# Transformer scores on 64 rows: queries and keys as exact halves in float32r, projected transposed, with their maxima turned by TensorE

## The chip, the core and the metric

One core of a Trainium2 chip runs the whole program. Its engines work side by side: TensorE (PE) multiplies matrices and writes the result to PSUM (8 banks of 512 float32 on each of 128 partitions), VectorE (DVE) and ScalarE (ACT) empty PSUM into SBUF, GpSimd (POOL) works on SBUF alone, and SyncE (SP) issues most of the DMAs. Every engine takes its instructions in a fixed order and waits on semaphores. TensorE's array can be cut: four pieces of 32 rows or two of 64 rows work at once on matmuls with few rows, and four pieces of 32 columns on matmuls with few outputs. The metric is device time from the first to the last instruction, in microseconds; before the change it is 3513.88 us, the median of three runs (3512.74 to 3514.75).

## The reference, cut to what matters

The program is a chain of eight residual stages on x of shape [2, 512, 128]: slot attention, a mixture of experts, cross-attention, a LoRA feed-forward, a six-layer transformer, a quantised feed-forward, a second six-layer transformer of the same form, and a second mixture of experts. The change is in the two transformers, of which each layer is:

```python
NL, D, H, DFF = (6, 128, 16, 512)
HD = D // H                                   # 8 per head
def _attn(q, k, v, mask):
    scores = jnp.einsum('bqhd,bkhd->bhqk', q, k) / np.float32(np.sqrt(HD))
    scores = jnp.where(mask[:, None, None, :], jnp.float32(-jnp.inf), scores)
    w = jax.nn.softmax(scores, axis=-1)
    return jnp.einsum('bhqk,bkhd->bqhd', w, v)
for i in range(NL):
    xn = _adaln(x, noise_emb, n1_w[i], n1_b[i])
    q, k, v = jnp.split(xn @ qkv_w[i].T, 3, axis=-1)
    q, k = _rope(q.reshape(B, L, H, HD)), _rope(k.reshape(B, L, H, HD))
    x = x + _attn(q, k, v.reshape(B, L, H, HD), src_mask).reshape(B, L, D) @ so_w[i].T
    xn = _adaln(x, noise_emb, n2_w[i], n2_b[i])
    q = _rope((xn @ cq_w[i].T).reshape(B, L, H, HD))
    k = _rope((context @ ck_w[i].T).reshape(B, LC, H, HD))
    v = (context @ cv_w[i].T).reshape(B, LC, H, HD)
    x = x + _attn(q, k, v, ctx_mask).reshape(B, L, D) @ co_w[i].T
    xn = _adaln(x, noise_emb, n3_w[i], n3_b[i])
    h = jax.nn.gelu(xn @ f1_w[i].T + f1_b[i], approximate=False)
    x = x + (h @ f2_w[i].T + f2_b[i])
```

There are 2 sequences of 512 tokens (B, L), 154 context tokens (LC) and 16 heads of 8 numbers. A layer so has two own-attentions and two cross-attentions, one for each sequence.

## The kernel before

**An attention block** (class Block) belongs to one sequence and works on 16 heads in four groups of four (class Group). A score has only 8 products, so the four heads of a group lie on four stretches of 32 partitions of qT and kT, and four matmuls run on the array at once. Each group passes over its scores twice. `maximum` computes them with queries on the output's partitions, 512 keys (own) or two times 154 keys (cross) to a bank, and VectorE reduces each bank to the negated maxima of 128 queries. `close` turns these maxima with a VectorE transpose and puts them by four small DMAs into one of the 32 rows of qT, against a row of ones in kT. `exp` then computes the scores anew with keys on the output's partitions, where that row subtracts the maximum, and ScalarE writes the exponentials to tiles p. When all chunks of keys of a group are done (4 of 128, or 2 of 77), 16 or 8 matmuls with the values vp or vcp, 32 output columns for each head, add up into one bank; `finish` transposes it on VectorE, divides by the sum that a column of ones gave, and writes the tile a.

**Around the groups** `before` makes the normalised input xn (layer norm on VectorE with a power on GpSimd, four TensorE transposes, scale and shift on ScalarE into nrm_t) and projects it to keys and queries. A projection is four matmuls with tokens on the output's partitions; `rope` multiplies it by cosines and sines on VectorE (rope_a, rope_s) and joins them on GpSimd (turned); `to_rows` transposes 32x32 blocks on VectorE (rows) and sends them by four DMAs to the rows of qT or kT. `context` does the same for the keys of the context, by way of kcp, TensorE transposes and ScalarE copies to kcT. `after` turns a, projects it, adds it to Y and, in a cross block, does the feed-forward layer.

**The order** is worked out when the program is built. The transformer runs two chains, the maxima of all groups and, LAG = 22 steps behind, their exponents, and records every instruction. The class Plan then orders the recorded instructions of all engines by a model of their durations, of the buffers and of the array's shapes, with shifts by kind of instruction (SHIFTS, by names such as "sync dma_start qT<rows"), and flushes them: all these instructions have the one source line 413. In a transformer all eight PSUM banks are one pool, ms. The layer's weights lw are one tile of 2826 columns in two buffers, loaded by one DMA. Before the transformers, `fixtures` sets aside and clears the tiles that both keep (vp, vcp, kcp, qT, kT), and `fix` fills in the mask row and the row of ones.

Of the kernel before, what the change touches and what calls it, by code (L numbers as in the profile page):

```python
# [12 lines left out]
F32 = mybir.dt.float32  # L13
U32 = mybir.dt.uint32
# [8 lines left out]
B = 2  # L23
# [8 lines left out]
NEG = -1e30  # L32
NL, H, HD, HG = 6, 16, 8, 4
DFF = 512
# [13 lines left out]
for _n, _w in (("n1", 256), ("n2", 256), ("n3", 256), ("q", 128), ("k", 128), ("v", 128), ("so", 128),  # L48
               ("cq", 128), ("ck", 128), ("cv", 128), ("co", 128), ("f1", 512), ("f2", 512),
               ("nb", 6), ("f1b", 4)):  # L50
    LAYER[_n] = slice(_at, _at + _w)
    _at += _w
LAYER_W = _at
LEAD, LAG, STEP = 30.0, 22, 0.9
MASK, TOP = 1, 31
# [17 lines left out]
PAIRS = ((0,), (1,), (2,), (3,)), ((2,), (3,), (0,), (1,))  # L73
# [3 lines left out]
for _n, _w in (("iota", 512), ("iota_p", NT), ("cos", NT * 4), ("sin", NT * 4), ("cos_c", NC * 4), ("sin_c", NC * 4), ("mask_row", 1)):  # L77
    CONST[_n] = slice(_at, _at + _w)
    _at += _w
# [39 lines left out]
class Op:  # L119
# [4 lines left out]
    def __init__(self, plan, lane, method, a, k):  # L124
# [16 lines left out]
        if lane == "tensor":  # L141
            cols = self.out[0].free_size()
            one = 0.838 * cols
            self.takes, self.lands = (max(one, 107.0), 170.0) if method == "transpose" else (2 * max(one, 55.0), 170.0)
            lhs = self.ins[0]
            (rows, r), (cells, c) = self.span(lhs), self.span(self.out[0])
# [37 lines left out]
class Plan:  # L184
# [76 lines left out]
    def order(self):  # L261
# [50 lines left out]
        cells = [0.0] * 16  # L312
# [11 lines left out]
        def place(x):  # L324
# [12 lines left out]
            if op.cells:  # L337
                s = max(s, max(cells[c] for i in sets[x] for c in ops[i].cells)) if op.mode == mode else max(s, max(cells) + self.SWITCH)
            elif op.table and op.table != table and s - at[x] < self.PATIENCE:
                s += self.TABLE  # L340
            return s

        while len(out) < n:
# [11 lines left out]
            for i in sets[x]:  # L355
# [6 lines left out]
                if op.cells:  # L362
                    last = max(cells[c] for c in op.cells)
                    s = max(s, last)
# [36 lines left out]
    def flush(self):  # L401
        order, where = self.order()

        def put(x):

            if isinstance(x, bass.AP) and x.tensor.name in where:
                return bass.AP(self.rooms[x.tensor.name].places[where[x.tensor.name]].tensor, x.offset, x.ap)
            return x
# [8 lines left out]
class Kernel:  # L417
    def __init__(self, ctx, tc, io):
# [10 lines left out]
        self.ctx_tok = c.tile([CP, B * NC, D], F32, name="ctx_tok")  # L429
# [5 lines left out]
        self.k = c.tile([P, CONST_W], F32, name="k")  # L435
        nc.sync.dma_start(self.k, io["consts"])
# [9 lines left out]
        for stages, banks in (((self.context, self.stage0, self.stage1, self.stage2, self.fixtures, self.weights5, self.stage3, self.fix), wide), ((self.stage4,), deep),  # L446
# [58 lines left out]
    def add_back(self, dst, ps, bias=None, ev=1):  # L505

        nc = self.nc
        t = self.ln.tile([P, S], F32, name="back")
# [9 lines left out]
    def normed(self, b, src, name="nrm"):  # L518

        t = self.ln.tile([P, NT, D], F32, name=name)  # L520
        self.layernorm(t, src[:, b * NT:(b + 1) * NT, :], P, NT)
        return t
# [36 lines left out]
    def stage0(self):  # L559
        nc, X = self.nc, self.X  # L560
        scale = math.sqrt(D)
        with self.pool("s0", 1) as one, self.pool("s0w", 2) as two:
# [36 lines left out]
            with nc.stretch():  # L599
                for b in range(B):  # L600
                    tok = slice(b * NT, (b + 1) * NT)
                    nc.at(0.0)
                    slots = self.normed(b, X, name=f"slots{b}")
# [4 lines left out]
                    for it in range(3):  # L608
# [47 lines left out]
                        slots = self.normed(0, s1c, name=f"slots{b}")  # L656
# [17 lines left out]
    def one_hot(self, out, idx):  # L674

        self.nc.vector.tensor_tensor(out, self.k[:, CONST["iota"]][:, 0:8].unsqueeze(1).to_broadcast([P, T, 8]),
                                     idx.unsqueeze(2).to_broadcast([P, T, 8]), ALU.is_equal)
# [216 lines left out]

    def rope(self, pool, dst, ps, cos, sin, rows, n):

        nc = self.nc
        x = ps.rearrange("p (n g f) -> p n g f", n=n, f=4)
        a = pool.tile([P, NT, 2 * H, 4], F32, name="rope_a")[:rows, :n]
        s = pool.tile([P, NT, 2 * H, 4], F32, name="rope_s")[:rows, :n]  # L900
        nc.vector.tensor_tensor(a, x, cos.unsqueeze(2).to_broadcast([rows, n, 2 * H, 4]), ALU.mult)
        nc.vector.tensor_tensor(s, x, sin.unsqueeze(2).to_broadcast([rows, n, 2 * H, 4]), ALU.mult)
        a, s = (t.rearrange("p n (h two) f -> p n h two f", two=2) for t in (a, s))
        nc.gpsimd.tensor_tensor(dst[0], a[:, :, :, 0, :], s[:, :, :, 1, :], ALU.subtract)
        nc.gpsimd.tensor_tensor(dst[1], a[:, :, :, 1, :], s[:, :, :, 0, :], ALU.add)
# [21 lines left out]
    def fixtures(self):  # L927
# [3 lines left out]
        self.tf = self.ctx.enter_context(self.pool("tf", 1))  # L931
        self.Y = self.tf.tile([P, T, D], F32, name="Y")
        self.qT, self.kT, self.kcp, self.vp, self.vcp, self.mx = ([] for _ in range(6))
        for b in range(B):
            for lst, name, rows, shape in ((self.kcp, "kcp", CP, [NC, H, 32]), (self.vp, "vp", P, [NT, VW]), (self.vcp, "vcp", CP, [NC, VW]),
                                           (self.mx, "mx", P, [32])):
                t = self.tf.tile([rows, *shape], F32, name=f"{name}{b}")
                nc.gpsimd.memset(t, 0.0)
                lst.append(t)
            for lst, name in ((self.qT, "qT"), (self.kT, "kT")):  # L940
                lst.append(self.tf.tile([P, HG, S], F32, name=f"{name}{b}"))

    def fix(self):

        nc = self.nc
        with self.pool("fix", 1) as one:
            at = CONST["mask_row"].start
            fixed = one.tile([P, NT, HG, 32], F32, name="fixed")
            nc.gpsimd.memset(fixed, 0.0)
            nc.vector.memset(fixed[:, :, :, TOP:TOP + 1], 1.0)  # L950
            for b in range(B):
                nc.scalar.activation(self.qT[b].rearrange("p g s -> p (g s)"), self.k[:, at:at + 1].to_broadcast([P, HG * S]), AF.Identity)
                nc.vector.tensor_copy(fixed[:, :, :, MASK], self.mneg[:, b * NT:(b + 1) * NT].unsqueeze(2).to_broadcast([P, NT, HG]))
                ps = self.transposed(fixed.rearrange("p n g d -> p n (g d)"))
                for g in range(HG):
                    self.evac(self.kT[b][:, g, :], ps, g % 2)
                nc.vector.memset(self.kcp[b][:, :, :, TOP:TOP + 1], 1.0)
                nc.vector.tensor_copy(self.kcp[b][:, :, :, MASK], self.mneg_c[:, b * NC:(b + 1) * NC].unsqueeze(2).to_broadcast([CP, NC, H]))
# [3 lines left out]
    def transformer(self, layers, f2b):  # L962
# [7 lines left out]
        nc, X, k = self.nc, self.X, self.k  # L970
        cos = k[:, CONST["cos"]].rearrange("p (n f) -> p n f", f=4)
        sin = k[:, CONST["sin"]].rearrange("p (n f) -> p n f", f=4)
        cos_c = k[:CP, CONST["cos_c"]].rearrange("p (n f) -> p n f", f=4)
        sin_c = k[:CP, CONST["sin_c"]].rearrange("p (n f) -> p n f", f=4)
        Y, qT, kT, kcp, vp, vcp, mx = (getattr(self, n) for n in ("Y", "qT", "kT", "kcp", "vp", "vcp", "mx"))
        parts = self.parts
        with self.pool("tf1", 1) as one, self.pool("tf2", 2) as two, self.pool("tfp", 22) as many:
# [10 lines left out]

            def heads(ps, n):
                return ps.rearrange("p (n h d) -> p n h d", n=n, d=HD)  # L990

            class Layer:


                def __init__(me, l):
                    nc.at(turn[0])
                    me.w = w = two.tile([P, LAYER_W], F32, name="lw")
                    nc.sync.dma_start(w, layers[l])
# [3 lines left out]
                    for n in range(6):  # L1002
                        nc.tensor.matmul(ps[:, n * B:(n + 1) * B], lhsT=w[:, n * P:(n + 1) * P],
# [6 lines left out]
                    me.kcT = [None] * B  # L1010

                def W(me, name):
                    return me.w[:, LAYER[name]]
# [7 lines left out]
            class Block:  # L1021
# [6 lines left out]
                def to_rows(me, dst, ps):  # L1028

                    t = two.tile([P, NT, H, HD], F32, name="turned")  # L1030
# [572 lines left out]
```

## Time and profile before

| | before |
|---|---|
| median of three runs | 3513.88 us |
| span of the profiled execution | 3512.3 us |
| first transformer, stretch 740 to 2010 us | 1270 us |
| second transformer, stretch 2130 to 3410 us | 1280 us |
| busy over the span: TensorE, VectorE, ScalarE, GpSimd | 90%, 68%, 48%, 15% |
| mean granted TensorE clock | 0.923 |
| DMA of the span | 61.02 MB, 179496 packets |

A line of instructions names its source line, engine, operation and tiles (out<-in), then shapes, count, busy time in us and the mean of one in ns, and after the bar the time that its engine stood idle just before, with what ended it. `128*32` at a matmul are rows and columns of the array that it takes. A float32 matmul stands in the records as two MATMULs. A busy TensorE is one on which at least one matmul is under way; its ends are modelled, so two that overlap count once, and 90% busy is not 90% of what the array could do.

### The profile page before, as it was taken

Reading aid. Unit: us, or ns where it says so; the run is one execution under the profiler, and the core shown is the slowest. Engines: PE = TensorE matmul, PEld = TensorE weight load, DVE = VectorE, ACT = ScalarE, POOL = GpSimd, SP = SyncE. Lnnn points to the kernel's source line nnn. Section 1 sums busy time; section 2 is a strip of 40 time slices with the busy share of each in tenths; the row PEclk is TensorE's granted clock in tenths of the full one; section 3 lists DMA queues with packets and bytes.
Section 4 is the critical chain, followed back from the end, with each engine's and each line's share of the span. In section 5 each row is a group of like instructions: output and inputs, shape, how many; then the busy total and the mean of one; then the engine's idle time right before and its main releaser. Section 6 shows DMA issues by size and latency. Waiting matters only on the chain.

```text
span 3512.3 us, 56998 instructions
## 1 busy us (share of the span) xinstructions
PE 3172.6 (90%) x21674; PEld 1830.5 (52%) x21674; DVE 2399.5 (68%) x5745; ACT 1694.5 (48%) x3249; POOL 536.6 (15%) x489
## 2 busy tenths in 40 slices
PE   5598999889999999999999848999999999999966
PEld 3364444455555555555555525555555555555545
DVE  6614555558687777868778567778687777868744
ACT  1123545416555554645645423655455555645631
POOL 2203757510100101100010001010100101010010
PEclk8699999979899999999999867999999999999977
DMA  0000000020000100001000001000000100100011
GB/s 24 19 31 25 1 1 1 7 54 5 11 25 8 29 7 11 25 8 31 7 9 11 5 0 48 5 17 21 11 25 8 30 6 11 27 6 14 8 52 54
DMA packets 179496, 61.02 MB, mean 17 GB/s; under 512 B 169475, under 2 KB 173367, under 8 KB 177559
## 3 DMA queue, kind: packets, MB, share of 16 engines
q1 hardware_dynamic: 177400, 54.72, 6.9%
q8 instruction: 172, 2.82, 0.3%
q10 hardware_dynamic: 1519, 1.74, 0.1%
q0 software_dynamic: 304, 0.92, 0.1%
q14 instruction: 101, 0.83, 0.1%
HBM read 36.37 MB, written 0.52 MB: 11 GB/s over the span
## 4 chain that ended last, share of the span: by engine, by line
PE 67%; DVE 9%; issue 1%; DMA 1%; ACT 1%; SPq 1%; POOL 1%; POOLq 0%; DVEq 0%; ACTq 0%
PE ms L413 63%; PE ms L179 2%; DVE mx L413 2%; PE big L179 1%; DVE avT L413 1%; SPq L413 1%; DMA qT<-rows 1%; DVE aT L413 1%; DVE ln_st L413 1%; DVE gate L179 0%; DVE Y L413 0%; DVE a L413 0%; DVE nrm L413 0%; DVE rec L413 0%; POOL turned L413 0%
## 5 line engine op out<-in xcount | busy, mean ns | idle before, releaser
L413 ACT ACTIVATE p<-ms 128x512 f32<-128x512 f32 (+1 forms) x2304 | 1173.8, 619 | 660.3 <-PE ms L413 656.5
L413 DVE TENSOR_REDUCE mx<-ms 128x1 f32<-128x512 f32 (+2 forms) x2316 | 1277.2, 608 | 210.7 <-PE ms L413 195.6
L413 PE MATMUL ms<-qT,kT 32*128 32x512 f32 (+1 forms) x3096 | 805.3, 637 | 0.2
L413 PE MATMUL ms<-kT,qT 29*128 29x512 f32 x3072 | 744.8, 644 | 7.8 <-DMA kT<-rows 7.2
L413 PEld LDWEIGHTS ms<-qT,kT 32*128 32x128 f32 (+1 forms) x3096 | 344.1, 185 | 211.3 <-ACT p L413 59.1
L413 PEld LDWEIGHTS ms<-kT,qT 29*128 29x128 f32 x3072 | 352.8, 188 | 151.2 <-DVE mx L413 41.0
L413 POOL TENSOR_TENSOR ln_rs<-ln_ve,mhalf 128x4 f32<-128x4 f32 x96 | 97.2, 1015 | 1898.6 <-DVE ln_ve L413 1878.4
L413 PE MATMUL ms<-p,vp 128*32 128x512 f32 x3072 | 354.6, 602 | 0.0
L413 PE MATMUL ms<-kcT,qT 29*128 29x154 f32 x3072 | 341.2, 335 | 9.5 <-DMA qT<-rows 6.9
L413 PE MATMUL ms<-qT,kcT 32*77 32x512 f32 x1536 | 323.1, 618 | 8.0 <-DVE mx L413 8.0
L413 PEld LDWEIGHTS ms<-kcT,qT 29*128 29x128 f32 x3072 | 287.9, 202 | 54.6 <-issue 30.9
L413 DVE STREAM_TRANSPOSE avT<-ms 128x512 f32<-128x512 f32 x192 | 137.2, 715 | 250.2 <-PE ms L413 241.2
L413 POOL TENSOR_SCALAR p<-p,s 128x666 f32<-128x666 f32 x128 | 248.8, 1956 | 117.7 <-DVE s L413 117.7
L413 ACT ACTIVATE nrm_t<-ms,gb 128x512 f32<-128x512 f32 x72 | 56.0, 778 | 343.8 <-PE ms L413 326.7
L413 PEld LDWEIGHTS ms<-p,vp 128*32 128x32 f32 x3072 | 91.1, 111 | 227.9 <-issue 180.5
L413 PE MATMUL ms<-p,vcp 77*32 77x512 f32 x1536 | 180.4, 597 | 0.0
L413 PEld LDWEIGHTS ms<-qT,kcT 32*77 32x77 f32 x1536 | 116.4, 143 | 108.7 <-DVE mx L413 51.6
L413 PE MATMUL ms<-ident,nrm 128*128 128x128 f32 x344 | 80.1, 354 | 90.4 <-DVE nrm L413 90.4
L413 DVE TENSOR_REDUCE m<-big 128x1 f32<-128x666 f32 x128 | 104.1, 845 | 82.6 <-PE big L413 82.6
L413 ACT ACTIVATE p<-big,m 128x666 f32<-128x666 f32 x128 | 103.6, 814 | 116.9 <-DVE m L413 116.2
L413 POOL TENSOR_TENSOR turned<-rope_a,rope_s 128x256 f32<-128x256 f32 x144 | 101.0, 726 | 306.4 <-DVE rope_s L413 306.4
L413 PE MATMUL ms<-ident,p 128*111 128x128 f32 x768 | 114.1, 287 | 18.6 <-POOL p L413 16.9
(328 smaller groups left out, 3391.3 us busy)
## 6 DMA issues: line engine op xcount, KB each, us to landing
lw<-in_layers SPq DMA_DIRECT2D x12, 1413.0 KB
ew<-in_w SPq DMA_DIRECT2D x24, 512.0 KB
qT<-rows SPq DMA_DIRECT2D x192, 64.0 KB
qT<-mxT SPq DMA_DIRECT2D x768, 2.0 KB
kT<-rows SPq DMA_DIRECT2D x96, 64.0 KB
wkv<-in_wkv SPq DMA_DIRECT2D x1, 1024.0 KB
f2b<-in_f2b SPq DMA_DIRECT2D x12, 64.0 KB
rv<-in_rows POOLq DMA_DIRECT2D x1, 640.0 KB, 6.6
```

The source lines that it names most:

```text
L179: return getattr(getattr(self._plan.real, self._name), method)(*a, **k)
L413: getattr(getattr(self.real, op.lane), op.method)(*map(put, op.a), **{n: put(x) for n, x in op.k.items()})
```

## The change

*Halves.* Each projected query or key t is split on VectorE by a bit mask into `high = t & 0xFFFFF000` and on GpSimd into `low = t - high`, which is exact. A head now takes 64 rows: for each of its 8 numbers the rows hold the four combinations of high and low of q against high and low of k; two spare rows take the maximum's own halves and one the mask. qT, kT and kcT are float32r tiles of 128 x 8 x n: two heads of a pair on 64 partitions each, 8 pairs. A score matmul names float32r operands.

*Projection.* `to_rows` makes queries and keys with the tokens in the free dimension: two matmuls of 512 columns (the second with the weights' halves swapped) replace four of 128; two VectorE multiplications by `turns`, an addition on GpSimd, the mask on VectorE, a subtraction on GpSimd, and four DMAs of 16 x 8 x 512, which write each half twice.

*Maxima.* `close` collects 16 columns m, transposes them with TensorE to 16 x 128, splits them with two VectorE operations, and sends two DMAs.

*Values.* With AT_ONCE = 1 the four matmuls of a chunk of keys are issued right after the chunk's exponents; their bank is held from the first chunk on.

*Memory and weights.* The layer's weights come in five single-buffered parts, hT takes tiles of p, several helpers share tiles, kcT is kept for the whole run, and `fix` comes ahead of the weights of stage 5. The orders PAIRS of heads change, and the model of Plan gets a duration for float32r and a weight load that the next matmul waits for. SHIFTS is the same table.

```diff
+            def to_rows(dst, src, w, n, key):
+                ab = []
+                for i in range(2):
+                    ps = self.bank()[:, :n]
+                    nc.tensor.matmul(ps, lhsT=w[:, i * P:(i + 1) * P], rhs=src, start=True, stop=True)
+                    x = two.tile([P, S], F32, name=f"rope_{'as'[i]}")[:, :n]
+                    nc.vector.tensor_tensor(x, ps, self.turns[:, i, :n], ALU.mult)
+                    ab.append(x)
+                t, low = ab
+                nc.gpsimd.tensor_tensor(t, t, low, ALU.add)
+                high = two.tile([P, S], F32, name="high")[:, :n]
+                nc.vector.tensor_scalar(high.bitcast(U32), t.bitcast(U32), HIGH, None, ALU.bitwise_and)
+                nc.gpsimd.tensor_tensor(low, t, high, ALU.subtract)
+                for half, x in enumerate((high, low)):
+                    for copy in range(2):
+                        first = 4 * copy + half if key else 4 * half + copy
+                        nc.sync.dma_start(dst.bitcast(F32)[first:P:8], x)
...
-                            r, t = slice(32 * j, 32 * j + TOP - 2), n * x + i
-                            nc.tensor.matmul(ps[j][:, i * nk:(i + 1) * nk], lhsT=q[r, t * P:(t + 1) * P], rhs=kT[r, :], start=True, stop=True)
+                            r, t = slice(64 * (j % 2), 64 * (j % 2) + TOP), n * x + i
+                            pair = 2 * me.g + j // 2
+                            nc.tensor.matmul(ps[j][:, i * nk:(i + 1) * nk], lhsT=qT[me.block.b][r, pair, t * P:(t + 1) * P], rhs=me.block.kT[r, pair, :],
+                                             start=True, stop=True)
...
-                    r = two.tile([P, 32], F32, name="mxT", bufs=3)
-                    nc.vector.transpose(r, mx[me.g % 2])
-                    to = me.block.qT[me.g][TOP:P:32].rearrange("j (n a q) -> j n a q", n=NT, q=32)
-                    for a in range(4):
-                        nc.sync.dma_start(to[:, :, a, :], r[32 * a:32 * a + 16])
+                    ps = self.bank(16)[:, :P]
+                    nc.tensor.transpose(ps, me.m, self.ident)
+                    r = two.tile([16, 2, P], F32, name="mxT", bufs=3)
+                    nc.vector.tensor_scalar(r[:, 0].bitcast(U32), ps.bitcast(U32), HIGH, None, ALU.bitwise_and)
+                    nc.vector.tensor_tensor(r[:, 1], ps, r[:, 0], ALU.subtract)
+                    for half in range(2):
+                        to = qT[me.block.b].bitcast(F32)[TOP + half:P:64, 2 * me.g:2 * me.g + 2, :]
+                        nc.sync.dma_start(to.rearrange("j g (n q) -> j (g n) q", q=P), r[:, half])
...
-                        r = slice(32 * j, 32 * j + 32)
-                        nc.tensor.matmul(ps[j][:rows], lhsT=kT[r], rhs=q[r, :], start=True, stop=True)
+                        r = slice(64 * (j % 2), 64 * (j % 2) + 64)
+                        nc.tensor.matmul(ps[j][:rows], lhsT=me.block.kT[r, 2 * me.g + j // 2, c * rows:(c + 1) * rows],
+                                         rhs=qT[me.block.b][r, 2 * me.g + j // 2, :], start=True, stop=True)
...
+                            if c == 0:
+                                me.av = self.bank()
+                            if (c + 1) % AT_ONCE == 0:
+                                nc.at(turn[0])
+                                with nc.together():
+                                    for c1 in range(c + 1 - AT_ONCE, c + 1):
+                                        for j in range(4):
+                                            at = (4 * me.g + j) * (HD + 1)
+                                            nc.tensor.matmul(me.av[32 * j:32 * j + 32], lhsT=me.block.vp[:rows, c1, at:at + 32], rhs=me.ps[c1][j][:rows],
+                                                             start=c1 == 0, stop=c1 == nch - 1)
...
-                    me.w = w = two.tile([P, LAYER_W], F32, name="lw")
-                    nc.sync.dma_start(w, layers[l])
+                    me.w = {}
+                    for i, names in enumerate(PARTS):
+                        lo, hi = LAYER[names[0]].start, LAYER[names[-1]].stop
+                        w = one.tile([P, hi - lo], F32, name=f"lw{i}")
+                        nc.sync.dma_start(w, layers[l][:, lo:hi])
...
+            for lst, name, n in ((self.qT, "qT", S), (self.kT, "kT", S), (self.kcT, "kcT", SC)):
+                t = self.tf.tile([P, HP, n], F32R, name=f"{name}{b}")
+                nc.gpsimd.memset(t.bitcast(F32), 0.0)
+                lst.append(t)
```

## The prediction

> **What bounds the kernel now.** I read the page's busy times first, then its costliest groups, then busy time by stretch, then the timeline inside a stretch.
>
> ```profile
> PE 3172.6 (90%) x21674; PEld 1830.5 (52%) x21674; DVE 2399.5 (68%) x5745; ACT 1694.5 (48%) x3249; POOL 536.6 (15%) x489
> L413 ACT ACTIVATE p<-ms 128x512 f32<-128x512 f32 (+1 forms) x2304 | 1173.8, 619 | 660.3 <-PE ms L413 656.5
> L413 DVE TENSOR_REDUCE mx<-ms 128x1 f32<-128x512 f32 (+2 forms) x2316 | 1277.2, 608 | 210.7 <-PE ms L413 195.6
> ```
>
> TensorE (PE) is busy 90%, and ScalarE (ACT) and VectorE (DVE) mostly wait for it. But a busy matmul is a latency, so I look at how densely they start, in one layer of the first transformer: its own-attention, the change to cross-attention, the feed-forward chain, the rest. The last two lines are both transformers whole.
>
> ```profile
> 985.00:1085.00 100.00, 99.34 (x701) 54.26 (x704) 83.96 (x178) 60.55 (x116) 9.39 (x12) 1.00 0.11 25
> 1085.00:1130.00 45.00, 44.05 (x408) 24.46 (x400) 28.31 (x77) 29.59 (x59) 3.17 (x5) 1.00 0.05 8
> 1130.00:1165.00 35.00, 30.37 (x239) 22.06 (x240) 24.63 (x73) 13.51 (x22) 6.20 (x8) 0.90 0.05 8
> 1165.00:1191.00 26.00, 25.93 (x184) 12.15 (x181) 22.21 (x44) 11.99 (x27) 0.00 (x0) 1.00 0.09 14
> 740.00:2010.00 1270.00, 1222.04 (x9076) 703.19 (x9080) 957.31 (x2204) 690.36 (x1326) 110.47 (x142) 0.94 0.08 16
> 2130.00:3410.00 1280.00, 1225.55 (x9121) 700.22 (x9120) 959.74 (x2212) 697.35 (x1335) 113.06 (x145) 0.95 0.08 17
> ```
>
> Columns: length, busy PE, PEld (weight loads), DVE, ACT, POOL, granted clock, DMA. DVE is at 84% in own-attention, 63% in the next 45 us. The two transformers are 2540 us of the 3512.3 us span.
>
> ```profile
> 997.32 3.84 PE L413 MATMUL ms<-lw,hT 128*128 128x128 f32 x32
> 1007.35 3.64 PE L413 MATMUL ms<-p,vp 128*32 128x512 f32 x32
> 1010.93 0.66 PE L413 MATMUL ms<-ident,nrm 128*128 128x128 f32 x4
> 1135.37 2.35 PE L413 MATMUL ms<-kcT,qT 29*128 29x154 f32 x28
> ```
>
> These give the density. A matmul is two records. The 32 of p,vp run four at a time: (3.64-0.59)/7 = 0.436 us per four, 0.11 per record, 0.22 per 512-column matmul on a quarter of the array. The 128-column ones start every 0.115, the 154-column ones every (2.35-0.29)/27 = 0.076. From the last p,vp start (1010.40) to the next shape 0.53 passes: 0.09 lost per change of array shape. At 1007 no score matmul starts for 3.6 us while DVE empties its banks.
>
> So TensorE's dense sum over both transformers: own scores 3072 x 0.22 = 676, cross maxima 1536 x 0.153 = 235, cross exponents 768 x 0.22 = 169, values 2304 x 0.22 = 507, the rest (2400 records x 0.11, 192 x 0.436, small ones) 379: 1966, plus 733 shape changes x 0.09 = 66, so 2032 (80% of 2540). DVE has 1917 (75%). Two engines of nearly equal load, in bursts: neither reaches its floor.
>
> **The change, part by part.** *Scores.* 5376 score matmuls go to one float32r pass on 64 rows: two at once instead of four. The trace has no float32r. Dearest row: an f32 pair on 64 rows (640 ns a record, two records each) is 0.436 x 2 per pair, 0.44 per matmul, twice today's. Cheapest: the 128-column weight load that each still needs; it starts every 0.076 at best with four row groups, 0.115 with one. One record instead of two on half the array is 0.22 per matmul, exactly today's; one record of half length is 0.11. I take 0.11, nearest to the load row. Scores become 5376 x 0.11 = 591 instead of 1080: -489.
>
> [...]
>
> *Values* are issued after each chunk of keys, not after the group: the built order changes array shape 1593 times, not 733: +860 x 0.09 = +77. In exchange the 3.6 us burst becomes four of 0.9, which DVE's buffered banks cover.
>
> *Projections.* 144 matmuls of 512 columns replace 286 of 128: +126-63; transposes of maxima +21, those of kcp and half of the context's fall away -13: +71. TensorE: 2032-489+77+71 = 1691.
>
> *DVE.* Each of 192 groups loses a 0.205 transpose (mxT) and gets two operations on 16x128 from PSUM; nearest rows 0.17 to 0.34, I take 0.25: +57. Each of 72 q or k turns loses a 0.705 transpose and gets a 128x512 mask; the row of a 77x512 TENSOR_SCALAR says 0.48: -16. Context +1. So DVE 1917 becomes 1959: now the largest. ACT loses 96 kcT copies, 20 us, and its 1387 us stay off the path.
>
> *Queues.* SP gives 384 instead of 768 DMAs of maxima (0.52 each), nothing waits behind them. Each q or k turn sends four of 256 KB instead of four of 64 KB. At the 147 GB/s that stood at a DMA share of 0.41, all engines move 360 GB/s: 1 MB takes 2.9 us, not 0.7. POOL does two 128x512 operations of 1.26 per turn (row Y<-Y,f2b) instead of two of 0.73: +1.1. Weights come in five single buffers; f1 and f2 are free a whole own-attention before they are needed: nothing.
>
> *Setup.* POOL memsets grow by 17,760 columns (qT, kT, kcT and masks in, kcp and mx out); the row of 0.95 us per 1024 gives 16.5. The third stage's ln_rs is queued behind them (694.3 now), but its transposes wait until 703.1 for other things: +12 to +17, I take +13.
>
> *Sum for a layer of 206 us.* Own-attention: DVE 84 + 8 groups x 0.3, less 0.9, is 85.5; TensorE there falls by 8 x 3.5 and gets 8 x 0.8 of changes. At 95% DVE, 90 instead of 100: -10 (bounds -14 at 100%, 0 if DVE stays at 84%). Next 45: TensorE loses 5 (22 lagging exponents, 64 maxima): -5 (0 to -12, where ACT's 29.6 and DVE's 28.3 stop it at 33). The chain of 35 us gets longer, since nothing covers it: POOL +1.1, projection 1.74 for 0.88 +0.9, DVE -0.2, transfer +2.2: +4 (+1 if the parts overlap, +8 if k and q come one after the other). Rest: 22.2/0.95: -2.6. Sum -13.6; 12 layers -163. With setup: 3512.3-163+13 = 3362 of span; the median of the runs is 1.6 above the span: 3364, so 3360.
>
> [...]
>
> **The rivals.** *A, larger gain (0.20).* Spread values keep DVE at 95% outside the chain, and the chain does not grow: (162.6-24.6)/0.95 + 35 = 180 per layer, -26 x 12 + 13: 3215. For: DVE is at 100% where scores are ready. Against: eight banks, one now held for values all the time.
>
> *B, the clock takes most of it (0.15).* Where TensorE is 45% busy (between the transformers) the clock is 0.65; in the chain 87% and 0.90; elsewhere 97% and 1.00.
>
> ```profile
> 2010.00:2130.00 120.00, 54.42 (x197) 0.65 0.07 26
> ```
>
> Thinner work may pull the chain's 0.90 to 0.65: 30.4 x (0.90/0.65-1) = +11.7 per layer, 140 in all: 3500. [...]
>
> *C, slower (0.18).* DVE becomes the bound and keeps its present idle share, since some of SHIFTS's entries are keyed to names such as qT<-rows that no longer occur. 1959/0.755 = 2595, +55, +13 setup, +4 x 12 chain: 3630; if the chain's part is inside the share, 3582. It decides if DVE in own-attention stays under about 86%. For: bursts remain in the chain. Against: the values burst, the largest cause, is cut in four. The same side is reached if a float32r matmul costs over (2032-1100)/5376 = 0.17.
>
> *D, nothing (0.04).* Gains and chain cancel: 3513.
>
> **How the numbers follow.** Forecast 0.43 (its own range 3280 to 3440), A 0.20, B 0.15, C 0.18, D 0.04. Faster by over 0.2% (about what a measurement tells from none): 0.43+0.20+0.15 = 0.78; within 0.2%: 0.04; slower 0.18. Range: low end 3190, A at its cheapest; high end 3540, into C: what is left out is most of C and a little of A, 0.18.
>
> **What would show it.** Right: float32r records of about half length, 0.11 apart; DVE above 90% in own-attention and the largest wait; a layer of about 192 us; chain stretch of 39; ln_rs of the third stage near 710. Wrong: scores 0.22 apart, a granted clock under 0.85 in the transformers, or DVE still waiting for PE a fifth of the time.

## The result, and the profile after

| | before | after |
|---|---|---|
| median of the runs | 3514.32 us (4 runs) | 3722.01 us (4 runs, 3700.93 to 3733.77) |
| span of the profiled execution | 3512.3 us | 3732.0 us |
| mean granted TensorE clock | 0.923 | 0.834 |

The ratio is 1.0575, 95% interval 1.0529 to 1.0621: slower, where 3360 us were forecast. First the page of the changed kernel, busy times and the five groups that answer to those shown of before.

```profile
PE 3166.4 (85%) x16014; PEld 1598.8 (43%) x16014; DVE 2484.7 (67%) x5961; ACT 1685.3 (45%) x3149; POOL 638.9 (17%) x494
...
L421 ACT ACTIVATE p<-ms 128x512 f32<-128x512 f32 (+1 forms) x2304 | 1189.8, 602 | 848.9 <-PE ms L421 826.4
L421 DVE TENSOR_REDUCE m<-ms 128x1 f32<-128x512 f32 (+1 forms) x2304 | 1265.8, 607 | 234.1 <-PE ms L421 230.8
L421 PE MATMUL ms<-qT,kT 64*128 64x512 f32 (+1 forms) x1560 | 554.6, 496 | 45.3 <-DMA qT<-mxT 27.2
L421 PE MATMUL ms<-kT,qT 62*128 62x512 f32 x1536 | 511.5, 503 | 73.7 <-DMA qT<-rope_s 39.1
L421 PE MATMUL ms<-p,vp 128*32 128x512 f32 x3072 | 464.8, 677 | 0.0
```

There are 5660 records fewer on TensorE (16014 for 21674), and still ACT waits for it longer than before (826 for 657 us) and DVE too (231 for 196). The scores' lines now show idle time of TensorE itself, ended by DMAs.

The windows of one layer of the first transformer follow (length, busy PE, PEld, DVE, ACT, POOL, granted clock, DMA share, GB/s), then both transformers whole.

```profile
1002.00:1040.00 38.00, 31.01 (x110) 16.40 (x110) 26.09 (x63) 10.12 (x15) 3.30 (x3) 0.70 0.14 35
1040.00:1165.00 125.00, 114.05 (x654) 48.86 (x654) 103.07 (x224) 74.99 (x144) 11.95 (x11) 0.94 0.15 38
1165.00:1202.00 37.00, 32.63 (x160) 17.39 (x157) 23.91 (x68) 14.40 (x28) 4.65 (x6) 0.63 0.17 39
1202.00:1227.00 25.00, 22.93 (x135) 10.95 (x133) 12.85 (x34) 16.50 (x30) 6.13 (x5) 1.00 0.27 65
760.00:2130.00 1370.00, 1213.05 (x6287) 568.22 (x6287) 998.86 (x2336) 692.07 (x1281) 157.15 (x145) 0.84 0.16 40
2260.00:3630.00 1370.00, 1196.45 (x6282) 563.16 (x6282) 986.83 (x2312) 700.30 (x1305) 150.98 (x141) 0.83 0.16 40
```

The layer takes 225 us, not 206. In own-attention (second line) DVE is at 103.07/125 = 82%, where it was at 84%: the values are spread and DVE is no fuller. Between the same two marks in both kernels, the first turned aT of a layer and its first score against the context's keys, own-attention takes a median of 125.4 us over ten layers, where it took 100.9; the forecast had 90. In the stretches before and after it the granted clock is 0.70 and 0.63; in both transformers it is 0.83 to 0.84, where 0.94 to 0.95 stood.

Was a score dearer than assumed? The timeline of TensorE in own-attention, at full clock:

```profile
1087.36 0.28 PE L421 MATMUL ms<-ident,m 128*16 128x128 f32 x1 [0.30 <-DVE m L421]
1087.57 0.50 PE L421 MATMUL ms<-qT,kT 64*128 64x512 f32 x2
1087.90 0.40 PE L421 MATMUL ms<-kT,qT 62*128 62x512 f32 x2
1088.14 0.81 PE L421 MATMUL ms<-qT,kT 64*128 64x512 f32 x2
```

No. A score is one record now, and a pair on the two halves of the array starts 1088.14 - 1087.90 = 0.24 us before the next pair: 0.12 us a matmul, where 0.11 was taken. What is new stands in brackets: the transposed maxima wait for DVE's last reduction, and in TensorE's order the scores queue behind them. The timeline at a layer's start shows two more such places.

```profile
1005.67 0.80 PE L421 MATMUL ms<-kT,qT 62*128 62x512 f32 x2 [4.87 <-DMA qT<-rope_s]
1006.40 2.07 PE L421 MATMUL ms<-lw,aT 128*128 128x128 f32 x8
...
1008.40 1.94 PE L421 MATMUL ms<-kT,qT 62*128 62x512 f32 x8
...
1012.19 1.10 PE L421 MATMUL ms<-ident,nrm 128*128 128x128 f32 x4 [0.38 <-DVE nrm L421]
...
1014.16 2.07 PE L421 MATMUL ms<-nrm_t,lw 128*128 128x512 f32 x2 [0.87 <-ACT nrm_t L421]
```

The first score of own-attention stands 4.87 us on the turned queries' DMA, and the projection lw,aT, whose aT was turned by 1002.9, stands behind it. After that the clock is at half (granted 0.50 from 1005.67 to 1008.40): eight lw,aT take 2.07 us, where they take 1.13 at full clock (at 1095.91, granted 1.00); two nrm_t,lw records take 2.07 us. The view of TensorE's waits over both transformers sums this up, the kernel before in the last four lines:

```profile
PE ms L421 <- DVE m L421: 84.1, 162, 1.2
PE ms L421 <- DMA qT<-mxT: 52.6, 30, 3.0
PE ms L421 <- DMA qT<-rope_s: 39.6, 9, 5.6
...
PE ms L421 <- DVE nrm L421: 37.2, 32, 7.8
...
PE ms L413 <- DVE nrm L413: 33.8, 16, 7.8
...
PE ms L413 <- DVE mx L413: 10.3, 23, 1.1
...
PE ms L413 <- DMA qT<-rows: 6.9, 12, 1.3
...
PE ms L413 <- DMA qT<-mxT: 0.6, 1, 0.6
```

The columns are us in total, times, longest. Turned keys made TensorE wait another 7.2 us in the kernel before.

A count of my own adds it up. Each matmul record gets the time in which its columns stream: at full clock 0.43 us for 512 columns of an f32 record (the 0.436 between two rounds of p,vp), half of it, 0.21, for a float32r one (an estimate; pairs start 0.24 apart), divided by the granted clock at its start. From 760 us on, the time in which anything streams, what of it exists only because the clock was below full, and the time in which nothing streams are, in us:

| kernel | something streams | of it added by the clock | nothing streams |
|---|---|---|---|
| before | 2330 | 122 | 423 |
| after | 1966 | 355 | 1006 |
| before, no table (below) | 2422 | 140 | 444 |
| after, no table | 1901 | 289 | 976 |

At full clock the streaming falls from 2330 - 122 = 2208 to 1966 - 355 = 1611: 597 us are saved. The clock gives back 233 and idle time 583: 219 more in all, as the spans differ.

Not all of this lies where the change is. The last stage, whose instructions the change does not touch, ran almost wholly at half clock in this profiled execution:

```profile
3472.69 1.95 PE L179 MATMUL big<-hT,ew 128*128 128x64 f32 x16
...
3666.38 3.62 PE L184 MATMUL big<-hT,ew 128*128 128x64 f32 x16
```

From its first xin,ew matmul to the end it takes 68.9 us, where it took 42.6. So it is in 3 of the 20 profiles of this case (59.5 us or more at half clock); the other 17 have 42.6 to 43.1. So a profiled execution can be 26 us longer for no reason that lies in the change, and a median may hold part of that (only one execution of each kernel has a trace). The stages of the profiled executions, in us; the kernels of the last six rows are those of the experiments below:

| kernel | first score at | first to last score, both transformers | last stage |
|---|---|---|---|
| before | 769.1 | 2472.7 | 42.6 |
| after | 795.8 | 2636.7 | 68.9 |
| before, no table | 770.5 | 2586.7 | 42.6 |
| after, no table | 794.6 | 2567.0 | 42.6 |
| after, names mended | 791.2 | 2556.3 | 42.6 |
| names mended, fillers | 795.2 | 2523.2 | 68.9 |
| names mended, no turned DMAs | 769.3 | 2463.2 | 42.6 |
| before, no turned DMAs | 746.3 | 2461.8 | 68.9 |

Of the 220 us between the first two spans, 164 lie in the transformers, 27 ahead of the first score and 26 in the last stage.

### The profile page after: what moved, and what is told of

Read it like the earlier page. It is cut to its first block, busy times and chain, and to the rows that moved or that the text cites. A ratio compares the mean times of both kernels' runs of the same rounds, so it can differ in the third digit from the quotient of the medians.

```text
span 3732.0 us, 46718 instructions
## 1 busy us (share of the span) xinstructions
PE 3166.4 (85%) x16014; PEld 1598.8 (43%) x16014; DVE 2484.7 (67%) x5961; ACT 1685.3 (45%) x3149; POOL 638.9 (17%) x494
## 5 line engine op out<-in xcount | busy, mean ns | idle before, releaser
L421 DVE TENSOR_REDUCE m<-ms 128x1 f32<-128x512 f32 (+1 forms) x2304 | 1265.8, 607 | 234.1 <-PE ms L421 230.8
L421 PE MATMUL ms<-qT,kT 64*128 64x512 f32 (+1 forms) x1560 | 554.6, 496 | 45.3 <-DMA qT<-mxT 27.2
L421 PE MATMUL ms<-kT,qT 62*128 62x512 f32 x1536 | 511.5, 503 | 73.7 <-DMA qT<-rope_s 39.1
L421 PE MATMUL ms<-p,vp 128*32 128x512 f32 x3072 | 464.8, 677 | 0.0
L421 PEld LDWEIGHTS ms<-qT,kT 64*128 64x128 f32 (+1 forms) x1560 | 251.6, 201 | 353.3 <-issue 124.9
L421 PEld LDWEIGHTS ms<-kT,qT 62*128 62x128 f32 x1536 | 231.1, 207 | 269.5 <-issue 107.7
L421 PE MATMUL ms<-nrm_t,lw 128*128 128x512 f32 x480 | 286.9, 741 | 21.8 <-ACT nrm_t L421 20.1
L421 PEld LDWEIGHTS ms<-kcT,qT 62*128 62x128 f32 x1536 | 230.9, 251 | 131.6 <-issue 76.2
L421 PE MATMUL ms<-kcT,qT 62*128 62x154 f32 x1536 | 268.3, 348 | 2.3 <-DVE m L421 0.6
L421 PE MATMUL ms<-qT,kcT 64*77 64x512 f32 x768 | 207.5, 485 | 29.2 <-DMA qT<-mxT 25.4
```

The source lines that it names most:

```text
L421: getattr(getattr(self.real, op.lane), op.method)(*map(put, op.a), **{n: put(x) for n, x in op.k.items()})
```

## The experiments

All ratios are to the kernel before, run beside each kernel on the same chip. Differences in us between two versions are of medians that can come from two chips; by the ratios they come out up to 16 us smaller or larger.

**1. Is it the order?** SHIFTS moves instructions of a kind ahead or back in the planner's order, by name. Eleven of its names no longer occur in the changed kernel: reductions are `m<ms`, not `mx<ms`; hT is p; rows and turned are gone. Five kernels. The first two empty the table in the kernel before and in the changed one:

```diff
-SHIFTS = {
-    "tensor matmul ms<aT,lw": -75.36, "tensor matmul ms<hT,lw": -2, "tensor matmul ms<kT,qT": 0.5,
...
+SHIFTS = {
+}
```

> The kernel before with the whole table of urgencies (SHIFTS) emptied; nothing else. Order theory (the table is fitted to the kernel before, and eleven of its entries name operations that no longer exist, so the change lost its order): the table is worth much, 3600 to 3750 us without it. Clock, chain and turn theories (the loss of 208 us comes from work and waits of the change itself): the table is worth little, 3500 to 3550.

> The changed kernel with the table of urgencies emptied; nothing else. Only its ratio to the kernel before with an empty table counts: this is the change without fitted orders on either side. Order theory: under 1.02. The other theories: 1.04 or more, as between the two kernels with the table (1.0575).

Measured: 3639.95 us, ratio 1.0365 (1.032 to 1.041), and 3655.1 us, 1.0405 (1.0378 to 1.0433). Two things follow. The table is worth 123 us to the kernel before, and it costs the changed one 67 (3722 against 3655). And with no table on either side the change is worth nothing: 3655.1/3640.0 = 1.004, with intervals that overlap. By stage, its transformers are then 20 us shorter (2567.0 for 2586.7), and what comes ahead of the first score is 24 us longer. This compares one order with one other, and an order alone can move the time by more than that (see 2).

The next gives the lost entries back under their new names; the one after it takes them from the kernel before:

```diff
-    "vector tensor_reduce mx<ms": -13.62,
...
+    "vector tensor_reduce m<ms": -13.62, "vector tensor_scalar mxT<ms": 18.22, "vector tensor_tensor mxT<ms,mxT": 18.22,
+    "scalar activation p<ms,lw": -13.16, "tensor matmul ms<p,lw": -2, "sync dma_start kT<high": -3.04,
...
```

> The changed kernel with the lost entries given back under the new names: the reductions of maxima -13.62, the two operations that split the maxima 18.22, the Gelu of the feed-forward -13.16 and its matmuls -2, the rotation's POOL and DVE operations -4.31 and 0.23, the DMAs of keys -3.04 and of queries 6.36. Order theory: at least half of the 208 us comes back, 3620 or less. Other theories: 3680 to 3740, since the waits stay.

> The kernel before with only those entries taken out of its table that no longer match in the changed kernel (eleven: reductions and turn of maxima, Gelu, feed-forward's second matmuls, rotation, turned rows, their DMAs, the context's keys). Order theory: at least 100 us are lost, 3610 or more. Other theories: under 3540.

Measured: 3627.58 us (1.0323, 1.0299 to 1.0347) and 3611.11 us (1.0271, 1.0247 to 1.0295). Giving them back wins 94 us, a little under half of the loss (in the transformers 80 of 164 us, half); taking them from the kernel before costs it 94 (3516.7 beside it). One entry alone, that of the reductions:

```diff
+    "vector tensor_reduce m<ms": -13.62,
```

> The changed kernel (3722 us) with one lost entry given back under its new name, that of the reductions of maxima (-13.62), which starts them ahead of VectorE's other work. If this entry carries the loss: 3620 to 3650, as with all twelve given back (3628). If the loss lies in the rotation, the DMAs or the feed-forward: 3690 to 3730.

Measured: 3649.56 us (1.0415, 1.0351 to 1.0479): 72 of the 94 us, and 58 of the 80 in the transformers. TensorE's waits in this run, beside those above:

```profile
PE ms L447 <- DVE m L447: 86.4, 173, 1.2
PE ms L447 <- DMA qT<-rope_s: 45.9, 23, 5.9
...
PE ms L447 <- DMA qT<-mxT: 4.6, 2, 3.0
```

Waiting for the maxima's DMA falls from 52.6 to 4.6 us; the other two stay. This fits that without its entry a reduction gave way to VectorE's other work, so that the maxima reached qT late and TensorE stood on them with the exponents' scores. The kernel with all entries back, 3628 us, is the base of what follows ("names mended" in the table of stages).

**2. Would better numbers in the planner's model help?** It was told what the traces show of the DMA link (212 GB/s over the eight transfers of keys and queries; the first of them, 256 KB issued at 993.60, landed at 996.75, 3.15 us later, of which 210 bytes per ns take 1.25), and of the clock (in windows of 3.41 us of both traces, by the share of the time in which something streams in the count above: of the full-speed windows followed by another the lowest has 0.38, of the half-speed windows followed by one at full speed the lowest has 0.76; but some 39 of 138 falls came after a share above 0.40):

```diff
-                slow.append(use[-1] < self.ENOUGH)
+                slow.append(use[-1] < (0.77 if slow[-1] else 0.40))
...
+                if op.lane == "sync":
+                    link = max(link, s + op.takes) + op.out[0].nbytes() / 210.0
+                    done = link + 2000.0
```

> The changed kernel with the lost entries given back (3628 us), its planner told two things that the traces measure: DMAs share one link of 210 bytes per ns and land 2 us later, and the clock falls to half after a window under 0.40 and returns only after one over 0.77. Order theory (the loss sits in an order planned with wrong times): 3500 to 3590. Clock and chain theories (the time is in the work and waits themselves): within 25 us of 3628.

> The changed kernel with the lost entries given back (3628 us) and the planner told of the shared DMA link only, not of the clock's two thresholds (both together: 3891 us). If the clock model did the harm: 3560 to 3640. If the link model did it: 3800 or more. If any other order is that much worse than a fitted one: in between, 3680 to 3800.

The link alone: 3627.42 us (1.0319, 1.0286 to 1.0352), no change. Both: 3890.83 us (1.1062, 1.1008 to 1.1115). So adding the planner's two numbers for the clock to the link costs 263 us, with the same instructions and only their order changed (these two alone were not run). No case of the first expectation foresaw that, the second did; why that order is so poor was not followed up.

**3. Values after each chunk, maxima by TensorE.** The two parts of the change in which I suspected harm were undone, each alone, on the base:

```diff
-                            if c == 0:
+                            if c == nch - 1:
                                 me.av = self.bank()
-                            if (c + 1) % AT_ONCE == 0:
...
-                                    for c1 in range(c + 1 - AT_ONCE, c + 1):
+                                    for c1 in range(nch):
```

> The changed kernel with the lost entries given back (3628 us), and the values issued at the end of a group, as in the kernel before, instead of after each chunk of keys. Values theory (860 more changes of shape, a bank held all the time, seven left): 40 us or more are won, 3590 or less. What the prediction assumed (a burst starves VectorE, spread values do not): 20 to 80 us are lost, 3650 to 3710.

```diff
-                    nc.tensor.transpose(ps, me.m, self.ident)
+                    nc.vector.transpose(t, me.m)
...
+                        for a in range(4):
+                            nc.sync.dma_start(to[:, :, a, :], r[32 * a:32 * a + 16, half])
```

> The changed kernel with the lost entries given back (3628 us), and the maxima turned by VectorE in 32x32 blocks, as before, and then split: no transpose of maxima on TensorE, eight DMAs of maxima for a group instead of two. Turn theory (TensorE waits in order for the last reduction, 113 us of idle time ahead of those transposes, and the scores queue behind it): most of it comes back, 3515 to 3570. Other theories: within 25 us of 3628.

Values at the group's end: 3788.84 us (1.0771, 1.0703 to 1.0838), 161 us worse. Maxima by VectorE: 3733.21 us (1.0597, 1.0542 to 1.0651), 106 us worse. Both are dearer than any case had it, and both parts help. TensorE's waits for the reductions, the longest of all in the view above, are cheaper than what avoids them here (a VectorE transpose and six more DMAs for a group); the turn theory falls. (Each of these changes the planned order as well; what an order is worth was seen in 2.)

**4. The chain from projection to scores.** A turn now sends 1 MB. First with one copy of each half, then with three of the four DMAs:

```diff
-                    for copy in range(2):
+                    for copy in range(1):
```

> The changed kernel with the lost entries given back (3628 us), and each turned half sent to one row of its head instead of two: two DMAs of 256 KB per turn instead of four. What is left out: the second copies of the high and low halves, so that the products of high with low halves are missing from the scores. Chain theory (1 MB per turn, 2 MB for keys and queries together in 11.5 us): 5 us or more in each layer, 3570 or less. Other theories: 3605 to 3630.

```diff
-                    for copy in range(2):
+                    for copy in range(2 - half):
```

> The changed kernel with the lost entries given back (3628 us), with three DMAs of 256 KB per turn instead of four: the row that holds low half times low half stays zero. What is left out: that product, some 2^-24 of a score. Chain theory: half of what two DMAs fewer won (48 us), 3595 to 3612. If the transfer does not set the wait but the first landing does: 3620 to 3635.

> The two runs before this one together: planner with the measured link and clock, and three DMAs per turn. If both theories hold and add up: 3470 to 3570. If only one of them: 3595 to 3612. If neither: 3620 or more.

Measured: 3579.48 us (1.0159, 1.0107 to 1.0212), 48 us less; 3613.09 us (1.0296, 1.023 to 1.0362), 14 us less, inside its interval; and with the planner of 2 3904.76 us (1.1096, 1.1043 to 1.115), which shows only the planner's harm again. Half of the volume, which is also half of the DMAs, is worth 48 us, 4 in each of 12 layers, where the chain theory had 5 or more.

Then both kernels with no such DMA at all, so that no score waits for projection, rotation or transfer:

```diff
-                for half, x in enumerate((high, low)):
+                for half, x in enumerate((high, low) if n < S else ()):
...
-                    for a in range(4):
+                    for a in range(0):
```

> The changed kernel with the lost entries given back (3628 us), without the DMAs that bring the turned keys and queries of the 512 tokens to their rows; what is left out: these keys and queries, so that scores are those of zeros and masks, and no score waits for projection, rotation or transfer (the maxima's DMAs stay). Chain theory (the gain is there and the chain eats it): 3350 or less, 278 us or more below, and a larger fall than that of the kernel before. Throughput theory (VectorE, clock and TensorE's order set the time anyway): 3500 to 3600.

> The kernel before (3514 us) without its DMAs of turned keys and queries; what is left out: these keys and queries, as in the run beside it. Chain theory: TensorE is 97 per cent busy outside the chain and hides most of it, so 60 to 170 us are won, 3340 to 3450. Throughput theory: as much as in the changed kernel, in per cent.

Measured: 3478.6 us (0.9888, 0.9859 to 0.9918) and 3469.04 us (0.984, 0.9792 to 0.9889). The chain costs the changed kernel 149 us and the kernel before 46 (60 to 170 were expected), 103 more. The profile of the second has the last stage at half clock, so part of its 26 us may stand in the 46; without the last stage the two profiled executions win 147 and 64 us, 83 apart. So the chain costs the changed kernel 7 to 9 us more in each layer, as the chain theory says; but the 3350 or less that it expected are not there. With no chain in either, the transformers are level again (2463.2 and 2461.8).

**5. The clock.** Matmuls that compute nothing of use were put into TensorE's idle gaps: 442 in the base (16898 records for 16014, two each; the expectation's count of 393 is too low), 133 in the kernel before, and 663 in the kernel with three DMAs.

```diff
+                    for _ in range(FILL.get(self.count, 0) if fresh and self.warm else 0):
+                        self.real.tensor.matmul(bass.AP(x.tensor, 0, [[512, P], [1, 256]]), lhsT=self.warm[0], rhs=self.warm[1], start=True, stop=True)
```

> The changed kernel with the lost entries given back (3628 us), and 393 matmuls of 256 columns that compute nothing of use, put ahead of those instructions of TensorE that started more than 0.5 us after the one before them, some 0.6 of each such gap. Clock theory (TensorE streams too little, and the dense work after each gap runs at half the clock): the granted clock rises from 0.847 to 0.89 or more and the time falls by 50 to 150 us, 3480 to 3580. Other theories: the added work lies in idle time or in the way, 3620 to 3700.

> The kernel before with 133 matmuls of 256 columns that compute nothing of use, put into 0.6 of its own 66 gaps of TensorE of over 0.5 us: the control for the same filling of the changed kernel, which won 42 us. Clock theory: the kernel before runs at 0.93 in its transformers and has little to win, 3495 to 3525. If filling helps any kernel alike: 3470 to 3480.

> The changed kernel with the lost entries given back, three DMAs per turn (3613 us; low half times low half is left out), and 663 matmuls of 256 columns that compute nothing of use in 0.8 of its own gaps of over 0.3 us. Clock theory: the two gains add up, granted clock 0.90 or more, 3540 to 3580. If the fillers now stand in the way: 3600 or more.

Measured: the base 3585.72 us (1.017, 1.0116 to 1.0225) at granted clocks of 0.886 to 0.898, 42 us less (50 to 150 in the clock theory); the kernel before 3488.17 us (0.9912, 0.9887 to 0.9936) at 0.943, 27 us less than the 3515.65 beside it; three DMAs and 663 fillers 3602.85 us (1.0273, 1.0224 to 1.0321) at 0.911, 10 less than without them, inside the interval. The windows of the two transformers in the first of these (its profiled execution, 3616.83 us, is the longest of five, with the last stage at half clock):

```profile
760.00:2000.00 1240.00, 1182.00 (x6380) 576.12 (x6379) 957.43 (x2227) 657.07 (x1220) 149.49 (x139) 0.91 0.18 43
2260.00:3450.00 1190.00, 1136.81 (x6304) 554.95 (x6301) 913.34 (x2147) 652.66 (x1208) 139.81 (x128) 0.93 0.17 40
```

The clock rises from 0.86 to 0.91 and 0.93 in these stretches, and DVE's busy time only from 948.23 to 957.43 and from 912.91 to 913.34. By the count of streaming time the clock's part up to the last stage falls from 312 to 198 us, 114 less, of which the transformers win 33 (2523.2 for 2556.3). So the half clock is real, and most of what it costs here lies beside other waits. It is also no matter of the changed kernel alone: filling won 27 us in the kernel before, more than the clock theory gave it (under 20) and less than the other (34 to 44).

**6. VectorE's path.** The maxima reduced over half of each row:

```diff
-                            nc.vector.tensor_reduce(to, ps[j][:, :n * nk].rearrange("p (i k) -> p i k", k=nk), AX.X, ALU.max, negate=True)
+                            nc.vector.tensor_reduce(to, ps[j][:, :n * nk].rearrange("p (i k) -> p i k", k=nk)[:, :, :nk // 2], AX.X, ALU.max, negate=True)
```

> The changed kernel with the lost entries given back (3628 us), its maxima reduced over the first half of each row of scores only; what is left out: the other half's part of the maxima (the scores, exponents and values are all computed). VectorE loses some 600 us of work. If VectorE's path sets the pace: 3250 or less. If TensorE's idle time, transfers and clock set it: 3500 to 3640.

Measured: 3470.59 us (0.9868, 0.9828 to 0.9909), 157 us less. The busy line of its page:

```profile
PE 2977.1 (86%) x16014; PEld 1534.5 (44%) x16014; DVE 1977.7 (57%) x5961; ACT 1678.9 (48%) x3149; POOL 639.0 (18%) x494
```

DVE's work fell from 2476.6 (its page in the base) to 1977.7, by 499 us, not 600; the time fell by a third of that. Between the two expectations: VectorE is on the path for part of the time, and no engine alone sets the pace.

**A version that beats both** is the kernel before with 133 fillers, 3488.17 us, 0.9912 of its time. No version of the changed kernel that leaves nothing out beats the kernel before.

## Why the prediction was wrong

*Scores, right.* 0.12 us a matmul for 0.11; the rival that needed over 0.17 by this way is out. TensorE's saving was not too small either: 597 us of streaming by my count.

*Values after each chunk, right in sign:* undoing it costs 161 us.

*DVE, small miss.* The two operations on the maxima take 0.28 each for 0.25; the mask 0.57 in the mean (median 0.42) for 0.48. In the two transformers' windows DVE has 69 us more (1985.7 for 1917.1), where 42 stood.

*POOL, right:* 1.28 us for 1.26.

*Setup, half of it.* The signpost came true: the third stage's ln_rs starts at 707.1 for 694.3, 12.8 us later where 13 stood. But the transposes that the term is about start 27.8 us later:

```profile
703.10 1.97 PE L179 MATMUL ms<-ident,nrm 128*128 128x128 f32 x8
...
730.87 1.97 PE L184 MATMUL ms<-ident,nrm 128*128 128x128 f32 x8
```

TensorE stands ahead of them on wq (from VectorE), and VectorE has three operations on record from 687.4 to 705.7, side by side and some 17.5 us each, beside POOL's memsets; in the kernel before each takes 1 us or less. The first score is 26.7 us late.

*Transfer, mis-sized.* "All engines move 360 GB/s: 1 MB takes 2.9 us". The packets of the eight DMAs of keys and queries, 2.1 MB, run from 994.84 to 1004.74: 9.9 us, 212 GB/s, 4.7 us per MB. The 147 GB/s from which the 360 came belonged to weights, in packets of 11304 bytes; these have 2048. The old transfer was mis-sized too: its packets run some 6 us (1162.5 to 1168.5) where 1.4 stood, so that the difference, some 4 us for keys and queries together, is not far from the +2.2.

*Chain, in its bounds:* "+4 (bounds +1 to +8)". From the start of aT in a layer's first cross block to the first score of the next own block 37.0 us (1132.84 to 1169.83) became 41.7 (963.93 to 1005.67), +4.7; the median of the ten changes of layer inside the transformers goes from 39.8 to 42.7. The runs without the transfers say 7 to 9, perhaps since the kernel before hides more of its chain; that is not shown.

*Own-attention, the step that failed on level terms.* "At 95% DVE, 90 instead of 100: -10." I took it that DVE fills up once TensorE is cheap, because DVE stood at 100% where scores were ready. It stands at 82%, and own-attention takes 125 us. Between the marks named with the result, the kernel with the names mended has 86% and takes 104, with no table 87% and 105 (the kernel before with no table: 83% and 94); so a better order brings part of this back and not the forecast. TensorE's saved time became idle time in TensorE's order, not work for DVE: at transposes, first scores and projections that each wait for another engine or a DMA, and hold up all behind them. With no table on either side the forecast's -154 us is +15, and its -163 for the transformers is -20. The "rest, 22.2/0.95" is the same assumption again. Taking 499 us from VectorE's emptying of PSUM won 157, so here that emptying is a part of the bound.

*The order, a term put at nothing.* I priced what the instructions cost and took their order as given. SHIFTS is one table for both kernels, and its names make it the kernel before's. The text saw that ("some of SHIFTS's entries are keyed to names ... that no longer occur"), put it into rival C at 0.18, and named the wrong entry, qT<-rows. The one that carried 72 of 94 us is the reductions'. By the runs the difference of 205 us (3722 against 3517) splits into 123 that the table is worth to the kernel before, 67 that it costs the changed one and 15 on level terms. That these three add up is no evidence, since they are steps from one kernel to the other by way of the two without a table; the evidence is each step's own pair of runs.

*Rivals.* C came true by its sign, its condition (DVE under 86%) and half of its reason, the lost names, at a price too low. The other half did not: DVE did not become the bound, its busy share of the transformers' windows fell from 75% to 72%. That C ended at 3630, the time with the names mended, is chance: its 3630 was for the names lost. B's signs are there: a granted clock of 0.83 to 0.84, and 0.63 in the chain's stretch, for which it had 0.65. By the count the clock adds 217 us of streaming up to the last stage; but what filling won back is 42 us, where B had 140, and filling took away only a part. A and D are out.

*Open:* how the 583 us of new idle time divide between chain, clock, VectorE and order. They overlap: each was relieved alone (42 to 157 us), not all together, and every edit also changes the planned order, which alone moved the time by 263 us. Whether the changed kernel would beat the kernel before with a table fitted to it was not tried.

## What to carry to other kernels

An order fitted to a kernel is part of its time: here 123 us of 3514. Before pricing a change, list the names by which hints, shifts or tables find their instructions, and see which of them still match. And a saving on an in-order engine at 90% busy is worth something only if what it waits for next is early (here 597 us of streaming were saved and 583 us of idle time came): price the waits at the heads of its queue, not only its sum and that of the next engine.

## What the runs showed of the hardware

*The clock fell after thin streaming, not only after silence.* The granted clock stands in the traces of both kernels as 1.0 or 0.5 (184 stretches in the changed kernel, 100 in the kernel before), and each stretch but the first and last of a trace lasts a whole multiple of 3.41 us. Over windows of that length, with the share of the array that streams as the measure (by my count): in both kernels no full-speed window with a share above 0.41 was followed by one at half speed, and no half-speed window under 0.65 by one at full speed. The two shares are bounds and not a switch: 25 full-speed windows of 0.41 or less stayed at full speed, and 104 half-speed windows over 0.65 stayed at half. Of the 92 full-speed windows in the changed kernel that were followed by a half-speed one, half had a share of 0.23 to 0.39, so something streamed in them. Only 7 of the 92 falls ended a silence of more than 3.41 us.

*Between the two shares, 0.41 and 0.65, the clock changed after no window of either trace.* The last stage, the same in all kernels, has, up to the 58 eo,put matmuls that end it, a share of 0.42 to 0.65 in its windows where it runs at full clock and of 0.50 to 0.68 where it runs at half. It ran at full clock in 17 profiles (42.6 to 43.1 us) and at half in 3 (68.9 us): in the changed kernel it is at half from one fall near its start, at 3665.6, and takes 26 us longer.

*Transfers from SBUF to SBUF.* Eight of 256 KB, issued within 6 us, brought 212 GB/s from the first packet to the last, some 60% of what the DMA share of the kernel before had suggested. Packets of 2048 bytes took a median of 156 ns in the changed kernel's trace, 84 in that of before, where none of them belongs to turned queries or keys.
